# Mask and row maximum of the diagonal score blocks as one VectorE instruction in a fused attention and FP4 feed-forward block

## The chip, the cores and the metric

The kernel runs on one core of a Trainium2 chip. The metric is device time in microseconds (us), median of three runs. A core has TensorE (PE in the profile; PEld is its weight load), VectorE (DVE), ScalarE (ACT), GpSimd (POOL) and SyncE (SP), which here issues the DMAs. SBUF is the working memory; PSUM has the banks into which TensorE writes.

## The reference

A transformer block with both branches on one normalised input; x is 8 x 1024 x 512, with 16 heads of 32 columns.

```python
xn = layernorm(x)
# causal attention
q, k, v = split(xn @ W_attn + b_attn)
att = (q @ k.T) * 32 ** -0.5
att = where(tril, att, -inf)
y   = softmax(att) @ v
a   = y @ W_proj + b_proj
# feed-forward: inputs and weights of each product rounded to blockwise FP4 (16 values a scale)
f   = fp4_linear(silu(fp4_linear(xn, w_gate)) * fp4_linear(xn, w_up), w_down)
out = x + a + f
```

## The kernel before

Tokens are taken in 64 tiles of 128 rows (8 batches of 8 tiles). Attention works in 64 units; a unit is two heads of one batch. Each unit takes two passes. `maxima` computes the scores with queries on the partitions and keeps each row's negated maximum (`neg`) and its sum of exponentials (`row_sums`). `weigh` computes the scores again, transposed (L710 adds the shift from the first pass, L713 the product), exponentiates them (L721), zeroes the masked half of diagonal blocks on POOL (L727) and multiplies by v (L692). Besides, `project` makes q, k and v (L464, L509), `network` is the feed-forward part (L817 products with gate and up, L795 product with down, L834 gating on DVE), `Quantised` rounds to FP4 in steps on DVE (L318 to L342), `transposed` turns the result on TensorE (L349) and copies it out on ACT (L350), and `finish` is the output projection (L922, L927). `weights_quantised` rounds the weights in the first part of the run.

In `maxima` a block is 128 query rows (tile t of the batch; t = 4 Q + i) against up to 512 keys (half h). Where h < Q the block is full, 512 columns, and there is no mask. Where h = Q it is diagonal and has n = (i + 1) x 128 columns, of which only the last 128 need the mask. Diagonal blocks of 128 and 256 columns hold both heads in one bank (`count` 2); those of 384 and 512 columns hold one head. Per unit that makes 8 full blocks and 12 diagonal ones, of 16 heads in all. `kind` says which of three statistics a block belongs to: 0 for Q = h = 0, 1 for the full blocks, 2 for Q = h = 1.

A block goes this way: matmul into a bank (L594); for a diagonal block the addition of the mask to the last 128 columns of each head, in place (L606); maximum over the columns, negated, into `neg` (L608); then `summed` exponentiates the bank in place on ACT with `neg` as bias, and the accumulator gives the row sum (L566). After that the bank is free. Six banks are shared by all parts of the kernel; two more hold the accumulators `y` and `acc`.

The order of all engines' instructions is fixed when the program is built. Each part is a generator; `merge` steps them by a planned clock. `dve`, `act` and `pool` add a planned cost to the time at which that engine is planned to be free. `Banks.take` gives the bank that is planned to be free first, and `expect` and `back` set that time. `Later` puts off an instruction to a due time. Of `maxima` these costs matter: 0.16 + 0.135 per head for the mask addition, 0.16 + 0.00103 per column for the reduce, and `LATE` = 0.6 from there to the exponentials; `yield cost, free["dve"] - QUEUE, 1` holds the next block back while DVE is planned to be more than `QUEUE` = 2 us behind. On the chip the engines run in these orders and wait for each other through semaphores. The planner's own costs are in microseconds, but no time of this document is taken from them.

At the end of a unit the statistics are put together (`least`, `gap`, `stat`), transposed (L641), copied to `statT` (L643) and stored to DRAM by two DMAs (L649, L652).

Of the kernel before, what the change touches and what calls it, by code (L numbers as in the profile page):

```python
# [9 lines left out]
F32 = mybir.dt.float32  # L10
# [4 lines left out]
ALU = mybir.AluOpType  # L15
AX = mybir.AxisListType
# [3 lines left out]
P = 128  # L20
# [3 lines left out]
MASKED = -1e30  # L24
# [3 lines left out]
def kernel(  # L28
# [31 lines left out]
    nc = tc.nc  # L60
# [14 lines left out]
    W = QG * P  # L75
# [17 lines left out]
    const = ctx.enter_context(tc.tile_pool(name="const", bufs=1))  # L93
    p1 = ctx.enter_context(tc.tile_pool(name="p1", bufs=1))
    p2 = ctx.enter_context(tc.tile_pool(name="p2", bufs=2))
# [9 lines left out]

    ident = const.tile([P, P], F32, name="ident")
    make_identity(nc, ident)
    mask = const.tile([P, P], F32, name="mask")
    make_causal_mask(nc, mask, mask_val=MASKED)
    power = const.tile([P, 1], F32, name="power")  # L110
    nc.gpsimd.memset(power, -0.5)

# [30 lines left out]
    def on(engine, us, after=0.0):  # L143

        free[engine] = max(free[engine], clock[0], after + HOP) + us
        return free[engine]

    def act(columns, after=0.0, function="other"):
        if function == "other":
            function = table[0]  # L150
        switch = TABLE if function != table[0] else 0.0
        table[0] = function
        return on("act", 0.17 + 0.00083 * columns + switch, after)

    def dve(us, after=0.0):
        return on("dve", us, after)
# [275 lines left out]
    def settle(entries):  # L432
        while entries:
            entries.pop(0).now()
# [120 lines left out]
    def maxima(un):  # L555

        NK = QG * HU

        neg = p2.tile([P, 3, NK], F32, name="neg")
        sums = p2.tile([P, 3, NK], F32, name="row_sums")  # L560
        older = []

        def summed(bank, sc, n, kind, k, count):
            for j in range(count):
                part = sc[:, j * n : (j + 1) * n]
                nc.scalar.activation(  # L566
                    part,
                    part,
                    AF.Exp,
                    bias=neg[:, kind, k + j : k + j + 1],  # L570
                    accum_out=sums[:, kind, k + j : k + j + 1],
                )
                end = act(n, 0.0, "exp") + 0.27
                free["act"] = end
            banks.back(bank, end)


        blocks = []
        for t in range(NT):
            for h in range(t // QG):  # L580
                blocks += [(t, h, (r,)) for r in range(HU)]
            if t % QG < 2:
                blocks.append((t, t // QG, range(HU)))
            else:
                blocks += [(t, t // QG, (r,)) for r in range(HU)]
        for t, h, heads in blocks:
            Q, i = t // QG, t % QG
            while len(un.qs) <= Q:
                yield 0.0, clock[0] + 0.5, 0
            n = W if h < Q else (i + 1) * P  # L590
            kind, k, count = Q + h, i * HU + heads[0], len(heads)
            bank, sc = banks.take()
            for j, r in enumerate(heads):
                nc.tensor.matmul(  # L594
                    sc[:, j * n : (j + 1) * n],
                    lhsT=un.qs[Q][:, r, i * P : (i + 1) * P],
                    rhs=un.ks[h][:, r, :n],
                    start=True,
                    stop=True,
                )  # L600
            cost = count * max(0.11, n * 0.000444)
            end = clock[0] + cost
            each = sc[:, : count * n].rearrange("p (r c) -> p r c", r=count)
            if h == Q:
                corner = each[:, :, n - P : n]
                nc.vector.tensor_tensor(corner, corner, mask.unsqueeze(1).broadcast_to([P, count, P]), ALU.add)  # L606
                end = dve(0.16 + 0.135 * count, end)
            nc.vector.tensor_reduce(neg[:, kind, k : k + count], each, AX.X, ALU.max, negate=True)  # L608
            end = dve(0.16 + 0.00103 * n * count, end)
            block = (bank, sc, n, kind, k, count)  # L610
            older.append(Later(end - clock[0] + LATE, lambda block=block: summed(*block)))
            banks.expect(bank, end + LATE + 0.6 + 0.4 * count)
            while len(older) > 3:
                older.pop(0).now()
            yield cost, free["dve"] - QUEUE, 1
        yield 0.0, end + LATE + 1.0, 0
        settle(older)

        least = p2.tile([P, NK], F32, name="least")
        nc.vector.tensor_tensor(least, neg[:, 1, :], neg[:, 2, :], ALU.min)  # L620
        gap = p2.tile([P, 2, NK], F32, name="gap")
        for part in range(2):
            nc.vector.tensor_tensor(gap[:, part, :], least, neg[:, 1 + part, :], ALU.subtract)
        yield 0.0, dve(0.6), 0
        nc.scalar.activation(gap, gap, AF.Exp)
        yield 0.0, act(2 * NK, 0.0, "exp"), 0
        nc.vector.tensor_tensor(sums[:, 1:, :], sums[:, 1:, :], gap, ALU.mult)
        nc.vector.tensor_tensor(sums[:, 1, :], sums[:, 1, :], sums[:, 2, :], ALU.add)

        high = p2.tile([P, 2, NK], F32R, name="neg_high")  # L630
        stat = p2.tile([P, 3, 2, HU, QG], F32, name="stat")
        by_head = lambda a: a.rearrange("p (i r) -> p r i", r=HU)
        for q, source in enumerate((neg[:, 0, :], least)):
            nc.vector.tensor_copy(high[:, q, :], source)
            nc.vector.tensor_copy(stat[:, 0, q], by_head(high.bitcast(F32)[:, q, :]))
            nc.vector.tensor_tensor(stat[:, 1, q], by_head(source), stat[:, 0, q], ALU.subtract)
            nc.vector.reciprocal(stat[:, 2, q], by_head(sums[:, q, :]))
        rows = 3 * 2 * NK
        yield 0.0, dve(2.0), 1
        bank, pt = banks.take()  # L640
        nc.tensor.transpose(pt[:rows, :P], stat.rearrange("p e q r i -> p (e q r i)"), ident)  # L641
        statT = p2.tile([rows, P], F32, name="statT")
        nc.scalar.copy(statT, pt[:rows, :P])  # L643
        end = act(P, clock[0] + 0.15)
        banks.back(bank, end)

        def store():
            un.shift = dram.tile([2, 2, HU, W], F32, name="shift_kept")
            nc.sync.dma_start(  # L649
                out=un.shift.rearrange("e q r (i p) -> (e q r i) p", p=P), in_=statT[: 2 * 2 * NK, :]  # L650
            )
            nc.sync.dma_start(  # L652
                out=un.batch.inverses[un.u].rearrange("q r (i p) -> (q r i) p", p=P), in_=statT[2 * 2 * NK :, :]
            )
            Later(3.0, load)

        def load():
            un.shT = shifts[un.n % 2]
            for q in range(2):
                for r in range(HU):  # L660
                    row = (q * HU + r) * HD
                    nc.sync.dma_start(out=un.shT.bitcast(F32)[row : row + 2, :], in_=un.shift[:, q, r, :])
            un.ready = clock[0] + 4.0

        Later(end - clock[0] + 0.5, store)
        yield 0.15, 0.0, 0
# [377 lines left out]
    with tc.manual_schedule(  # L1044
# [25 lines left out]
        part, late = EARLY * 0.25, [0.0]  # L1070
# [18 lines left out]
        def first_maxima():  # L1089
            yield 0.0, clock[0] + 6.0, 1  # L1090
            yield from maxima(units[0])
# [24 lines left out]
        def preparations():  # L1116
            for n in range(AHEAD, N, QT):
# [4 lines left out]
            [  # L1122
                Stream((weigh(un), 17.5, un.n, 1.0) for un in units),
                Stream((maxima(un), 6.0, un.n - 1 - SOONER, 1.0) for un in units[1:]),
                Stream(networks()),
                Stream((quantised(tl), 0.45, tl.n + LAG - 1, 0.5) for tl in tiles),
# [42 lines left out]
```

## Time and profile before

| | |
|---|---|
| median of 3 runs | 4298.45 us (4293.16 to 4298.53) |
| profiled execution | 4298.47 us |
| its span, first to last instruction | 4296.8 us |
| mean granted TensorE clock | 0.990 |
| instructions | 58518 |

A profile page gives the busy time of each engine, and groups of instructions: line, engine, operation, output<-input by the program's names, shapes and count; then, behind the first bar, the busy time and the mean duration in ns of one; behind the second bar the idle time of the engine just ahead of them, and what ended it. A list of waits gives for each pair (who waits <- for whom) the total us, how many times and the longest. Matmuls are pipelined and recorded longer than they occupy the array, so that the rows of PE add up to more than its busy time. Some records are missing: of 768 wide reduces 518.1 / 0.687 = 754 are seen.

### The profile page before, as it was taken

How to read it: one execution, taken by the hardware profiler on the slowest of the kernel's cores; microseconds unless marked ns; L12 is line 12 of the kernel's file. 1: busy time of each engine (PE TensorE's matmuls, PEld its weight loads, DVE VectorE, ACT ScalarE, POOL GpSimd, SP SyncE). 2: the span in 40 equal slices, each digit the busy share in tenths (PEclk: the TensorE clock that was granted, in tenths of full speed). 3: DMA queues.
4: the chain of work that ended last, by engine and by line, in shares of the span. 5: the costliest groups of instructions: out<-in, count | busy, mean ns of one | idle time of the engine just before them, and what ended most of it. 6: DMA issues, size and time to landing. Idle time of an engine off the chain costs nothing.

```text
span 4296.8 us, 58518 instructions
## 1 busy us (share of the span) xinstructions
PE 4145.0 (96%) x17684; PEld 2617.7 (61%) x17684; DVE 2942.0 (68%) x6811; ACT 2331.5 (54%) x5918; POOL 543.8 (13%) x1295
## 2 busy tenths in 40 slices
PE   7779999999999999999999999999999999999998
PEld 6665566666666666666666666666666555555555
DVE  6787766667676667676667676667676777767755
ACT  2246656565555555555555555555555566666640
POOL 0001111111111111111111111111111111111110
PEclk9889999999999999999999999999999999999999
DMA  5654434455454555454455454555454433333314
GB/s 182 173 170 129 123 102 119 118 154 162 130 157 139 141 165 163 126 162 133 140 165 163 127 161 133 143 160 163 128 151 126 114 87 92 92 85 94 94 53 125
DMA packets 564187, 573.85 MB, mean 134 GB/s; under 512 B 114976, under 2 KB 420128, under 8 KB 563872
## 3 DMA queue, kind: packets, MB, share of 16 engines
q1 hardware_dynamic: 563872, 570.10, 47.7%
q8 instruction: 143, 2.34, 0.2%
q14 instruction: 172, 1.41, 0.1%
HBM read 400.56 MB, written 169.35 MB: 133 GB/s over the span
## 4 chain that ended last, share of the span: by engine, by line
PE 80%; DVE 6%; ACT 4%; DMA 3%; issue 2%; SPq 1%; ACTq 0%; POOL 0%; DVEq 0%; POOLq 0%
PE bank L817 25%; PE acc L795 12%; PE bank L464 8%; PE y L692 7%; PE bank L710 6%; PE bank L713 6%; PE bank L922 5%; PE bank L594 4%; PE bank L509 4%; ACT bank L566 3%; PE bank L349 2%; DVE neg L608 2%; DMA inv_y<-inv_kept 1%; DVE scale L333 1%; DMA yT<-y_kept 0%
## 5 line engine op out<-in xcount | busy, mean ns | idle before, releaser
L608 DVE TENSOR_REDUCE neg<-bank 128x1 f32<-128x512 f32 (+3 forms) x1280 | 800.5, 635 | 258.5 <-PE bank L594 232.2
L566 ACT ACTIVATE bank<-bank,neg 128x512 f32<-128x512 f32 (+3 forms) x1536 | 857.9, 559 | 194.3 <-DVE neg L608 154.7
L721 ACT ACTIVATE pr<-bank 128x512 f32<-128x512 f32 (+3 forms) x1536 | 662.1, 495 | 377.0 <-PE bank L713 364.5
L727 POOL TENSOR_SCALAR_AFFINE_SELECT pr<-pr 128x128 f32<-128x128 f32 x1024 | 389.2, 393 | 3109.9 <-ACT pr L721 3103.6
L710 PE MATMUL bank<-shT,pick 128*128 128x512 f32 (+3 forms) x1536 | 678.3, 450 | 14.5 <-DMA shT<-shift_kept 12.3
L817 PE MATMUL bank<-wuT,xqT 128*128 128x512 f32 (+1 forms) x1536 | 672.4, 562 | 10.7 <-ACT bank L566 6.0
L795 PE MATMUL acc<-wdT,hqT 128*128 128x512 f32 x1408 | 665.2, 598 | 1.3 <-ACT hqT L350 1.3
L817 PE MATMUL bank<-wgT,xqT 128*128 128x512 f32 (+1 forms) x1536 | 666.1, 561 | 0.2 <-ACT bank L566 0.2
L594 PE MATMUL bank<-ks,qs 128*128 128x512 f32 (+3 forms) x1536 | 614.3, 467 | 32.6 <-ACT bank L566 29.9
L713 PE MATMUL bank<-qs,ks 128*128 128x512 f32 (+3 forms) x1536 | 516.9, 346 | 0.0
L606 DVE TENSOR_TENSOR bank<-bank,mask 128x128 f32<-128x128 f32 (+1 forms) x768 | 259.1, 337 | 350.2 <-PE bank L594 350.1
L594 PEld LDWEIGHTS bank<-ks,qs 128*128 128x128 f32 x1536 | 274.5, 190 | 243.9 <-issue 104.1
L817 PEld LDWEIGHTS bank<-wuT,xqT 128*128 128x128 f32 x1536 | 275.7, 190 | 211.8 <-issue 138.1
L817 PEld LDWEIGHTS bank<-wgT,xqT 128*128 128x128 f32 x1536 | 281.0, 190 | 195.9 <-issue 138.9
L710 PEld LDWEIGHTS bank<-shT,pick 128*128 128x128 f32 x1536 | 290.0, 189 | 173.9 <-issue 90.1
L476 ACT ACTIVATE full<-bank,bqk 128x256 f32<-128x256 f32 x256 | 107.3, 470 | 516.2 <-PE bank L464 367.5
L795 PEld LDWEIGHTS acc<-wdT,hqT 128*128 128x128 f32 x1408 | 257.5, 191 | 207.0 <-issue 196.6
L713 PEld LDWEIGHTS bank<-qs,ks 128*128 128x128 f32 x1536 | 290.3, 189 | 103.9 <-issue 70.6
L464 PE MATMUL bank<-xnT,wa 128*128 128x256 f32 x1536 | 347.5, 379 | 1.0 <-ACT xnT L350 0.5
L464 PEld LDWEIGHTS bank<-xnT,wa 128*128 128x128 f32 x1536 | 291.2, 190 | 75.7 <-issue 33.2
L692 PE MATMUL y<-pr,vs 128*32 128x512 f32 (+3 forms) x3072 | 315.8, 501 | 2.2 <-POOL pr L727 2.1
L566 ACT ACTIVATION_READ_ACCUMULATOR bank<-bank,neg 128x1 f32 x1536 | 313.3, 204 | 0.0
(97 smaller groups left out, 4539.7 us busy)
## 6 DMA issues: line engine op xcount, KB each, us to landing
wa<-in_L_attn_W_attn_dram SPq DMA_DIRECT2D x146, 512.0 KB
qs<-qk_kept SPq DMA_DIRECT2D x512, 128.0 KB
ks<-qk_kept SPq DMA_DIRECT2D x512, 128.0 KB
wp<-in_L_attn_W_proj_dram SPq DMA_DIRECT2D x81, 512.0 KB
qk_kept<-high SPq DMA_DIRECT2D x128, 256.0 KB
qk_kept<-full SPq DMA_DIRECT2D x128, 256.0 KB
y_kept<-yu SPq DMA_DIRECT2D x256, 128.0 KB
yT<-y_kept SPq DMA_DIRECT2D x112, 256.0 KB
```

What stands on the lines that cost most here:

```text
L464: nc.tensor.matmul(pq[:, j, :], lhsT=halves[j][:, c, :], rhs=xnT[:, c, :], start=(c == 0), stop=(c == NC - 1),)
L566: nc.scalar.activation(part, part, AF.Exp, bias=neg[:, kind, k + j : k + j + 1], accum_out=sums[:, kind, k + j : k + j + 1],)
L594: nc.tensor.matmul(sc[:, j * n : (j + 1) * n], lhsT=un.qs[Q][:, r, i * P : (i + 1) * P], rhs=un.ks[h][:, r, :n], start=True, stop=True,)
L606: nc.vector.tensor_tensor(corner, corner, mask.unsqueeze(1).broadcast_to([P, count, P]), ALU.add)
L608: nc.vector.tensor_reduce(neg[:, kind, k : k + count], each, AX.X, ALU.max, negate=True)
L692: nc.tensor.matmul(y[row : row + HD, q0:], lhsT=un.vs[h][:, jj, r * HD : (r + 1) * HD], rhs=pr[:, q0:], start=(j < 2), stop=(j >= last - 1 ...
L710: nc.tensor.matmul(w[:, q0:], lhsT=pick[:, Q * HU + r, :], rhs=un.shT[:, q0:], start=True, stop=False)
L713: nc.tensor.matmul(w[:, q0:], lhsT=un.ks[h][:, r, jj * P : (jj + 1) * P], rhs=un.qs[Q][:, r, q0:], start=False, stop=True,)
L721: nc.scalar.activation(pr[:, q0:], w[:, q0:], AF.Exp)
L727: nc.gpsimd.affine_select(out=pr[:, q0 : q0 + P], in_=pr[:, q0 : q0 + P], compare_op=ALU.is_ge, fill=0.0, base=0, pattern=[[1, P]], channe ...
L795: nc.tensor.matmul(tl.acc, lhsT=job.hqT[:, j, :], rhs=wdT[:, i, :], start=(i == 0), stop=(i == NI - 1))
L817: nc.tensor.matmul(job.g, lhsT=job.tl.xqT[:, c, :], rhs=wT[:, c, job.i0 : job.i0 + job.w], start=(c == 0), stop=(c == NC - 1),)
```

## The change

The mask becomes 512 columns wide: 384 columns of zeros and then the causal mask of 128. A diagonal block's head then takes one `tensor_tensor_reduce`: it adds the last n columns of the wide mask to the n columns of scores, multiplies by -1, writes this back to the bank, and takes the minimum of it into `neg`, which is the negated row maximum as before. Since the bank now holds negated scores in the diagonal blocks (`kind` 0 and 2), the exponential there takes `scale=-1.0`. Full blocks keep their reduce. The planned cost of a diagonal head is 0.16 + 0.00105 per column. `statT` moves from a pool with two buffers to one with one.

```diff
-    mask = const.tile([P, P], F32, name="mask")
-    make_causal_mask(nc, mask, mask_val=MASKED)
+    mask = const.tile([P, W], F32, name="mask")
+    nc.gpsimd.memset(mask[:, : W - P], 0.0)
+    make_causal_mask(nc, mask[:, W - P :], mask_val=MASKED)
...
                     bias=neg[:, kind, k + j : k + j + 1],
+                    scale=1.0 if kind == 1 else -1.0,
                     accum_out=sums[:, kind, k + j : k + j + 1],
...
-            each = sc[:, : count * n].rearrange("p (r c) -> p r c", r=count)
             if h == Q:
-                corner = each[:, :, n - P : n]
-                nc.vector.tensor_tensor(corner, corner, mask.unsqueeze(1).broadcast_to([P, count, P]), ALU.add)
-                end = dve(0.16 + 0.135 * count, end)
-            nc.vector.tensor_reduce(neg[:, kind, k : k + count], each, AX.X, ALU.max, negate=True)
-            end = dve(0.16 + 0.00103 * n * count, end)
+                for j in range(count):
+                    part = sc[:, j * n : (j + 1) * n]
+                    nc.vector.tensor_tensor_reduce(
+                        part,
+                        part,
+                        mask[:, W - n :],
+                        scale=-1.0,
+                        scalar=3e38,
+                        op0=ALU.add,
+                        op1=ALU.min,
+                        accum_out=neg[:, kind, k + j : k + j + 1],
+                    )
+                    end = dve(0.16 + 0.00105 * n, end)
+            else:
+                nc.vector.tensor_reduce(neg[:, kind, k : k + 1], sc[:, :n], AX.X, ALU.max, negate=True)
+                end = dve(0.16 + 0.00103 * n, end)
...
-        statT = p2.tile([rows, P], F32, name="statT")
+        statT = p1.tile([rows, P], F32, name="statT")
```

## The prediction

> **What bounds the kernel now.** I read the busy shares first, then the chain of work that ended last.
>
> ```profile
> span 4296.8 us, 58518 instructions
> ...
> PE 4145.0 (96%) x17684; PEld 2617.7 (61%) x17684; DVE 2942.0 (68%) x6811; ACT 2331.5 (54%) x5918; POOL 543.8 (13%) x1295
> ...
> PE 80%; DVE 6%; ACT 4%; DMA 3%; issue 2%; SPq 1%; ACTq 0%; POOL 0%; DVEq 0%; POOLq 0%
> ```
>
> TensorE (PE) is busy 4145 of 4297 us and carries 80% of the chain. VectorE (DVE), which the change works on, is busy 68%. So DVE time saved is worth nothing by itself; it is worth what PE stops waiting. The table of busy time by stage tells where PE waits:
>
> ```profile
> 0.00:107.00 107.00, 84.89 (x391) 73.04 (x392) 72.37 (x165) 24.63 (x51) 8.64 (x23) 0.97 0.58 182
> 107.00:215.00 108.00, 79.51 (x368) 69.17 (x367) 79.50 (x178) 24.77 (x58) 3.56 (x6) 0.84 0.61 174
> 215.00:322.00 107.00, 83.43 (x375) 64.82 (x377) 91.90 (x213) 48.69 (x138) 6.49 (x16) 0.89 0.57 170
> ...
> 1000.00:2000.00 1000.00, 989.68 (x4272) 628.32 (x4271) 679.37 (x1583) 565.15 (x1433) 133.07 (x309) 1.00 0.53 149
> 2000.00:3000.00 1000.00, 990.92 (x4261) 630.07 (x4260) 677.99 (x1573) 562.65 (x1429) 137.14 (x320) 1.00 0.54 150
> ```
>
> After start and length the columns are PE, weight loads, DVE, ACT (ScalarE), POOL. In the steady part PE idles about 10 us per 1000. All PE idle time in the span is 4296.8 - 4145.0 = 152 us, 74 of it in the first 322 us. No saving can go much above that. What PE waits for, from the list of waits:
>
> ```profile
> ACT bank L566 <- DVE neg L608: 154.7, 161, 3.0
> ...
> PEld bank L594 <- ACT bank L566: 89.9, 208, 3.3
> ...
> PE bank L594 <- ACT bank L566: 29.9, 93, 2.9
> ```
>
> This is the changed path: a score block is written to a PSUM bank (L594), masked (L606) and reduced (L608) on DVE, exponentiated in place on ACT (L566), and only then may PE write that bank again. PE's matmuls idle 29.9 us for it at L594 and, in smaller rows, 6.1 at L817 and about 2 elsewhere: 38 us. Its weight loads wait some 150 us on the same release (89.9 at L594, 29.7, 13.8, 11.1 and 8.6 elsewhere), most of it while an earlier matmul still streams.
>
> **The change part by part.** The DVE rows it touches, by shape:
>
> ```profile
> L608 DVE TENSOR_REDUCE neg<-bank 128x1 f32<-128x512 f32 x768 | 518.1, 687 | 240.9 <-PE bank L594 232.2
> ...
> L606 DVE TENSOR_TENSOR bank<-bank,mask 128x128 f32<-128x128 f32 x512 | 150.1, 293 | 197.2 <-PE bank L594 197.2
> ...
> L608 DVE TENSOR_REDUCE neg<-bank 128x1 f32<-128x384 f32 x256 | 142.7, 558 | 8.7
> ...
> L606 DVE TENSOR_TENSOR bank<-bank,mask 128x256 f32<-128x256 f32 x256 | 109.0, 426 | 153.0 <-PE bank L594 153.0
> ...
> L608 DVE TENSOR_REDUCE neg<-bank 128x2 f32<-128x512 f32 x128 | 88.5, 692 | 4.4
> ...
> L608 DVE TENSOR_REDUCE neg<-bank 128x2 f32<-128x256 f32 x128 | 54.3, 424 | 4.4
> ```
>
> *Removed.* All 768 mask additions, 259.1 us. The reduces of diagonal blocks: 142.7 + 88.5 + 54.3, and of the 768 wide reduces the 256 on diagonal blocks, 256 x 0.687 = 175.9. Together 720.5 us. The other 512 wide reduces stay.
>
> *Added.* One fused instruction per head and diagonal block: 16 for each of the 64 units (two heads of one batch), 256 each of 128, 256, 384 and 512 columns. The built program shows each as two DVE instructions, the streaming one and a one-column write of the accumulator into `neg`; so DVE gets 2048 + 512 instead of 768 + 1280 of these, 512 more. Neither is in the trace. For the streaming one the nearest rows also take one PSUM and one SBUF input: L606 at 128 columns 0.293, L927 at 256 0.416, L834 at 384 and 512 0.550 and 0.682, in sum 1.941, times 256 = 496.9 us. For the accumulator write the nearest is the one-column L398, 0.154: 1024 x 0.154 = 157.7. Sum 654.6 us, **66 us of DVE less** (2942 to about 2876). Bounds: a write that hides behind its stream costs 0, making 224 less. ACT's own accumulator read (204 ns at L566), with the 65 ns by which the accumulating 512-column L566 exceeds the plain L721 (666 against 601), gives 0.269 x 1024 = 275 and DVE 52 us more. If the fused form streamed at half rate, 256 x 1280 columns more at about 1.04 ns (L834, 132 ns for 128 columns) add 341: 275 us more. I take 0.154: same engine, one column, while L566's is another engine's.
>
> [...]
>
> *Path of one diagonal block.* Before: addition, a gap of 0.04 in the timeline, reduce: 0.29 + 0.04 + 0.69 = 1.02 us at 512 columns, 0.89 at 384, 1.16 and 0.89 for pairs of 256 and 128. After: 0.84, 0.70, 1.14, 0.89. Only the single-head blocks get shorter, by 0.18, and ACT and the bank follow. In each pair the second fused instruction waits for the first's accumulator write (a semaphore in the built program); behind it in DVE's queue stand the quantiser's steps, delayed by no more than the 0.04 that the removed wait cost.
>
> *The order.* The planner priced the old diagonal path at 0.98 for a 512 block (measured 1.02) and prices the new one at 0.16 + 0.00105 n, 0.70. So all queues come out in another order. In the built programs PE has the same matmuls, with 5829 instead of 5738 changes from line to line; weighting each kind of change by its mean delay in this trace gives 459 us instead of 465, so -6. Pricing PE's work between a score block's matmul and the next write to its bank by the trace's back-to-back matmuls (0.43 us for 512 fp32 columns, 0.23 for 512 fp32r), 100 of 1280 blocks get their bank rewritten within 2.5 us before, 35 after. The bank path needs about 2 us (1.02, then 0.67 + 0.20 on ACT, and hops), so these are the reuses on which PE waits. Fewer by 65 in 100: of the 38 us 25 go; were the weight loads' 150 us all exposed, 122 would. I take 25, near the lower end, as loads overlap matmuls.
>
> *Given back.* The plan is too early by what it does not price: 0.84 - 0.70 = 0.14 us for each of 1024 fused pairs, 143 us of lateness, against 0.04 x 768 = 31 before. Lateness reaches PE where the bank is wanted soon: 101 of 1280 reuses lie within 3.5 us, 8%, so 0.08 x 112 = 9 us; as ACT's queue is in order and the releases of other banks stand behind a late exponential, I add as much as half again, 4. Together 0.12 x 112 = 13. Ends: 0, and 112 x 0.25 = 28, where 0.25 is PE's 38 us over ACT's 154.7 us of waiting for L608.
>
> *At nothing.* POOL's additional fill of 384 columns at the start is about 0.4 us (L115's 512 take 0.52) and is covered by DVE's first wait for `xt`, 14.3 us; without it, 0.4. `scale` -1 on L566 is an immediate in the same instruction. `statT` with one buffer instead of two makes L643 wait for the previous unit's two stores, one unit (about 64 us) earlier; both lie 5 us behind L643 in the trace, and if uncovered would cost those 5 us per unit. Table loads stay 187.
>
> **Sum.** On the profiled 4298.47 us (span 4296.8 and 1.67 around it; the median is 4298.45, so no correction): -25 - 6 + 13 = -18. **4280 us**.
>
> **Rivals.** *The wait moves.* PE's floor is its own work; a removed wait is found again at another line in front of a PE at 99%. For it speaks the steady part's 10 us per 1000, against it the fewer tight reuses. Without the 25, -6 and +13 are left; at an unpriced few us either way I call it 0: 4298. *DVE saves nothing, the order still helps.* With 0.269 per accumulator write the lateness is 0.255 a block, 261 us, 230 over before: -31 + 0.12 x 230 = -3, or with the 8% alone -13; 4290. For it speaks ACT's row, against it that ACT is another engine. *Slower: the fused instruction streams at half rate* and DVE becomes late. Lateness is then 0.14 + 0.33 on average, 481 us, 450 over before; with the 0.25 share +113, with 12% +54, less 31: +23 to +82, likeliest +50, 4348 us. DVE would stand at 75%. It turns the sign where lateness times share passes 31 us: at the 12% share from (31 / 0.12 + 31) / 1024 = 0.28 us per block, twice my estimate. For it speaks that no row shows such an instruction; against it that L606 and L834 already stream two inputs at full rate.
> [...]
> *Also slower*: the new order itself puts a wait elsewhere (a quantiser step late on DVE, so its transposes L349 late on PE: 30.8 us in 6 waits before, almost all in the first stage); twice those waits give +30 - 18 = +12, 4310.
>
> **How the numbers follow.** Forecast 0.45, wait moved 0.17, DVE saves nothing 0.10, half rate 0.12, order worse 0.16. A measurement of this kernel can tell about 0.2%, 8.6 us, from no change. Faster: 0.45 and half of the 0.10, 0.50. Same: the 0.17 and the other 0.05, 0.22. Slower: 0.28. The low end: all 38 us of bank waits gone, the 6, nothing given back, and 12 of the loads' 150 us: -56, 4242. The high end takes in the order rival and the lower part of the half-rate one: 4335. The forecast's own range is 4242 to 4289.
>
> **What would show it.** Right: DVE near 2876 us, PE's idle behind L566 near 15 instead of 38, PE busy unchanged within 15. The streaming instruction at 512 columns near 0.68 and its accumulator write near 0.15 decide the price. Wrong: a 512-column stream over 1 us, or unchanged ACT bank waits, or more PE idle in front of L349 or L692.

## The result, and the profile after

| | before | changed |
|---|---|---|
| median, same chip | 4297.34 us (4293.16 to 4298.53) | 4256.54 us (4251.42 to 4260.17) |
| profiled execution, span | 4298.47, 4296.8 us | 4251.42, 4249.7 us |

The ratio is 0.9906, 95% interval 0.9893 to 0.9919: 41 us faster where 18 were forecast. Direction and range held; the size did not. The comparisons further down were made on other chips, whose medians for the kernel before lie between 4293.7 and 4301.0, so they are given as ratios; 0.001 is 4.3 us.

The profile page of the changed kernel, busy times and chain (its lines are shifted: L568 is the old L566, L597 the old L594, L724 the old L710):

```profile
span 4249.7 us, 58555 instructions
...
PE 4131.2 (97%) x17684; PEld 2619.1 (62%) x17684; DVE 2763.2 (65%) x7323; ACT 2321.8 (55%) x5918; POOL 546.5 (13%) x1296
...
PE 82%; ACT 7%; DVE 4%; DMA 1%; issue 1%; SPq 0%; ACTq 0%; POOL 0%; DVEq 0%
```

DVE has 512 instructions more and is busy 179 us less. PE is busy 13.8 us less with the same matmuls (the mean granted clock, 0.991 instead of 0.990, accounts for an estimated 0.001 x 4250 = 4 of that), and idle 4249.7 - 4131.2 = 118.5 us instead of 151.8. The table of busy time by stage, same columns as before:

```profile
0.00:107.00 107.00, 84.22 (x394) 72.98 (x395) 73.31 (x168) 24.79 (x52) 8.64 (x24) 0.97 0.59 184
107.00:215.00 108.00, 78.32 (x373) 68.33 (x372) 80.00 (x185) 25.28 (x59) 4.68 (x8) 0.87 0.62 175
215.00:322.00 107.00, 86.71 (x390) 65.93 (x389) 90.53 (x239) 52.23 (x147) 6.49 (x17) 0.87 0.56 171
...
1000.00:2000.00 1000.00, 996.24 (x4310) 632.77 (x4309) 635.00 (x1710) 560.36 (x1432) 135.28 (x314) 1.00 0.53 149
2000.00:3000.00 1000.00, 996.10 (x4277) 631.92 (x4276) 635.90 (x1703) 569.05 (x1452) 133.31 (x311) 1.00 0.54 151
```

PE now idles 4 us per 1000 in the steady part instead of 10. By the copies of `y` (two a unit on ACT, in the traces' order of time, units counted from 0), unit 8 begins to be copied out 10 us sooner (761 against 771), unit 48 26 us sooner (3304 against 3330), the last unit 57 us sooner (4098.5 against 4155.5). The very last copy comes 45 us sooner (4127 against 4172), and what follows it, feed-forward products and output projections, takes 122 us instead of 125. So the gain is spread over the run, and thickest in the last 15 units, where a unit takes about 53 us instead of 54 to 55.

The groups of the fused instruction, busy and mean as before:

```profile
L610 DVE CUSTOM_DVE_ANT_0 bank<-bank,mask 128x512 f32<-128x512 f32 x256 | 175.4, 701 | 99.7 <-PE bank L597 98.6
L610 DVE DVE_READ_ACCUMULATOR2_ANT neg<- 128x1 f32 x1024 | 144.6, 141 | 0.1
L610 DVE CUSTOM_DVE_ANT_0 bank<-bank,mask 128x384 f32<-128x384 f32 x256 | 142.9, 570 | 110.8 <-PE bank L597 110.3
L610 DVE CUSTOM_DVE_ANT_0 bank<-bank,mask 128x256 f32<-128x256 f32 x256 | 110.9, 433 | 37.6 <-PE bank L597 33.1
...
L610 DVE CUSTOM_DVE_ANT_0 bank<-bank,mask 128x128 f32<-128x128 f32 x256 | 76.1, 297 | 221.5 <-PE bank L597 213.6 <-ACT pr L735 3.6
```

The streams took 0.701, 0.570, 0.433 and 0.297 us; the forecast had 0.682, 0.550, 0.416 and 0.293. There is no half rate. The accumulator write is recorded at 0.141, near the 0.154 taken, yet it costs almost nothing, as the timeline of DVE shows (start, duration):

```profile
1511.64 0.56 DVE L610 CUSTOM_DVE_ANT_0 bank<-bank,mask 128x384 f32<-128x384 f32 x1
1512.11 0.14 DVE L610 DVE_READ_ACCUMULATOR2_ANT neg<- 128x1 f32 x1
1512.11 0.68 DVE L335 TENSOR_REDUCE scale<-hid 128x32 f32<-128x512 f32 x1
...
1503.12 0.14 DVE L610 DVE_READ_ACCUMULATOR2_ANT neg<- 128x1 f32 x1
1503.30 0.43 DVE L610 CUSTOM_DVE_ANT_0 bank<-bank,mask 128x256 f32<-128x256 f32 x1
```

The write starts before its stream's record ends (1511.64 + 0.56 = 1512.20), and the next instruction starts with it. It shows where the next one waits for it, above all at the second of a pair: 0.18 from its start to the next start. With the old cost of 720.5, a fall of 178.8 leaves 541.7 for the diagonal blocks; the streams, 256 x 2.001 = 512, leave 29 us, 0.03 per write.

PE's own waits, who waits <- for whom, total us, times, longest:

```profile
PE bank L597 <- ACT bank L568: 21.7, 55, 2.3
...
PE bank L655 <- DVE stat L651: 4.8, 1, 4.8
...
PE bank L724 <- ACT bank L568: 1.1, 2, 0.6
PE bank L831 <- ACT bank L568: 1.0, 4, 0.3
```

Behind the score banks PE idles 24 us instead of 38. Two waits of the end of a unit, which the forecast had not counted, also shrank: for the statistics to 4.8, and for the shift's load into `shT`, which is gone. The kernel before had

```profile
PE bank L641 <- DVE stat L637: 12.6, 9, 5.1
PE bank L710 <- DMA shT<-shift_kept: 12.3, 7, 3.1
```

These three, 14, 8 and 12 us, are about the whole 33 us by which PE idles less; with the 14 us of busy time they make the 47 us between the two spans. ACT's own waits for the maxima, on the other hand, are nearly what they were, 119.8 + 30.6 = 150.4 us instead of 154.7:

```profile
ACT bank L568 <- DVE neg L610: 119.8, 90, 2.8
...
ACT bank L568 <- DVE neg L622: 30.6, 34, 2.4
```

### The profile page after: what moved, and what is told of

It reads as the page before. It is cut to its first block, busy times and chain, and to the rows that moved or that the text cites. A ratio compares the mean times of both kernels' runs of the same rounds, so it can differ in the third digit from the quotient of the medians.

```text
span 4249.7 us, 58555 instructions
## 1 busy us (share of the span) xinstructions
PE 4131.2 (97%) x17684; PEld 2619.1 (62%) x17684; DVE 2763.2 (65%) x7323; ACT 2321.8 (55%) x5918; POOL 546.5 (13%) x1296
## 4 chain that ended last, share of the span: by engine, by line
PE 82%; ACT 7%; DVE 4%; DMA 1%; issue 1%; SPq 0%; ACTq 0%; POOL 0%; DVEq 0%
PE bank L831 26%; PE acc L809 12%; PE bank L466 8%; PE y L706 7%; PE bank L724 6%; PE bank L727 6%; PE bank L597 5%; PE bank L936 5%; PE bank L511 4%; ACT bank L568 3%; PE bank L351 2%; ACT L568 1%; ACT L843 1%; ACT pr L735 1%; DMA ks<-y_kept 1%
## 5 line engine op out<-in xcount | busy, mean ns | idle before, releaser
L568 ACT ACTIVATE bank<-bank,neg 128x512 f32<-128x512 f32 (+3 forms) x1536 | 856.7, 559 | 163.7 <-DVE neg L610 119.8
L610 DVE CUSTOM_DVE_ANT_0 bank<-bank,mask 128x128 f32<-128x128 f32 (+3 forms) x1024 | 501.2, 500 | 469.5 <-PE bank L597 455.7
L724 PE MATMUL bank<-shT,pick 128*128 128x512 f32 (+3 forms) x1536 | 683.8, 453 | 2.7 <-DVE hid L848 1.5
L597 PE MATMUL bank<-ks,qs 128*128 128x512 f32 (+3 forms) x1536 | 636.2, 475 | 24.7 <-ACT bank L568 21.7
L622 DVE TENSOR_REDUCE neg<-bank 128x1 f32<-128x512 f32 x512 | 345.7, 685 | 186.8 <-PE bank L597 185.6
L597 PEld LDWEIGHTS bank<-ks,qs 128*128 128x128 f32 x1536 | 277.5, 191 | 234.1 <-issue 111.3
L724 PEld LDWEIGHTS bank<-shT,pick 128*128 128x128 f32 x1536 | 290.4, 189 | 155.7 <-issue 78.9
L568 ACT ACTIVATION_READ_ACCUMULATOR bank<-bank,neg 128x1 f32 x1536 | 315.4, 205 | 0.0
```

The costliest lines, as they stand in the source:

```text
L568: nc.scalar.activation(part, part, AF.Exp, bias=neg[:, kind, k + j : k + j + 1], scale=1.0 if kind == 1 else -1.0, accum_out=sums[:, kind, ...
L597: nc.tensor.matmul(sc[:, j * n : (j + 1) * n], lhsT=un.qs[Q][:, r, i * P : (i + 1) * P], rhs=un.ks[h][:, r, :n], start=True, stop=True,)
L610: nc.vector.tensor_tensor_reduce(part, part, mask[:, W - n :], scale=-1.0, scalar=3e38, op0=ALU.add, op1=ALU.min, accum_out=neg[:, kind, k ...
L622: nc.vector.tensor_reduce(neg[:, kind, k : k + 1], sc[:, :n], AX.X, ALU.max, negate=True)
L724: nc.tensor.matmul(w[:, q0:], lhsT=pick[:, Q * HU + r, :], rhs=un.shT[:, q0:], start=True, stop=False)
```

## The experiments

The question: where do the other 23 us come from? **Theory A**: from the order, since a cheaper plan of the diagonal blocks redraws all queues. **Theory B**: from the shorter path of a block on the chip, at 512 columns about 0.75 instead of 1.02 us (stream and the end of its accumulator write). Two kernels take one each. They have, on PE, ACT and SP, exactly the order of the one kernel and the instructions of the other.

**The fused instruction in the order of before**

The edit is against the changed kernel; the first new line stands behind the loop over the heads.

```diff
-                    end = dve(0.16 + 0.00105 * n, end)
+                end = dve(0.16 + 0.135 * count, end)
...
-                end = dve(0.16 + 0.00103 * n, end)
+            end = dve(0.16 + 0.00103 * n * count, end)
```

> The fused instruction with the planned costs of the kernel before, so that every queue but VectorE's has the order of the kernel before. Theory A (the gain is the new order): within 10 us of the kernel before, some 4290, with PE still idle some 30 us behind L566 at L594. Theory B (the gain is the shorter path of a block, about 0.74 instead of 1.02 us at 512 columns): most of the 41 us, some 4265, and PE's idle behind the exponential near 20.

Measured 4292.06 us, ratio 0.9994 (0.9985 to 1.0003). DVE was busy 2780.0 us, 162 less than before, and that was worth nothing that can be measured. PE still idled behind the exponentials as before:

```profile
PE bank L597 <- ACT bank L568: 30.1, 93, 3.3
...
PE bank L724 <- DMA shT<-shift_kept: 11.1, 7, 2.4
```

**Mask addition and reduce in the order of the changed kernel**

This edit is against the kernel before.

```diff
-                end = dve(0.16 + 0.135 * count, end)
...
-            end = dve(0.16 + 0.00103 * n * count, end)
+            if h == Q:
+                for j in range(count):
+                    end = dve(0.16 + 0.00105 * n, end)
+            else:
+                end = dve(0.16 + 0.00103 * n, end)
```

> Mask addition and reduce as before, but planned at the fused instruction's cost, so that every queue but VectorE's has the order of the changed kernel. Theory A: 4265 to 4275, most of the gain without the fused instruction. Theory B: 4297 or slower. A third theory, that the two need each other: 4300 to 4320, since each diagonal block is about 0.28 us later than planned, 0.28 x 768 = 215 us of lateness, of which 8 to 12% reach the end.

Measured 4271.11 us, 0.9943 (0.9930 to 0.9957): 24 us of the gain without the fused instruction, against a plan that is wrong for what runs. PE's waits have the look of the changed kernel; none for `shT` is left:

```profile
PE bank L594 <- ACT bank L566: 22.3, 54, 2.7
```

The wait for the statistics is 7.0 us here. So B falls as the main cause and A holds, with this one pair of orders; whether the cheaper plan or chance made the new order better is asked below. But the fused instruction is worth something in an order made for it: 0.9943 to 0.9906 is 16 us, by the two intervals 8 to 24.

**Lateness priced**

```diff
+                    nc.vector.tensor_copy(extra, part[:, 0:1])
                     nc.vector.tensor_tensor_reduce(
```

The changed kernel gets a copy of one column of the block, to a tile of its own, ahead of each fused instruction.

> The changed kernel in its own order, with one more unplanned one-column copy from the block's bank on VectorE ahead of each fused instruction (1024, about 0.12 to 0.15 us each, 120 to 155 us of lateness). It prices lateness: by the 8 to 12% of the prediction 10 to 19 us slower than the changed kernel (4267 to 4275), by the 25% of its upper end 30 to 39 us (4287 to 4295). If lateness is absorbed by idle VectorE time: within 4 us.

Measured 4273.03 us, 0.9951 (0.9938 to 0.9963), 16 to 19 us slower than the changed kernel (medians, ratios). The copies take

```profile
L611 DVE COPY extra<-bank 128x1 f32<-128x1 f32 x1024 | 157.8, 154 | 405.3 <-PE bank L598 395.5
```

so 10 to 12% of unplanned DVE time on this path reaches the end; the intervals of the two ratios leave 7 to 17%. The 16 us above fit the same share: DVE was busy 2927.1 - 2763.2 = 164 us longer in the separate form.

**The storage alone**

```diff
+    wide_mask = const.tile([P, W], F32, name="mask")
+    nc.gpsimd.memset(wide_mask[:, : W - P], 0.0)
+    make_causal_mask(nc, wide_mask[:, W - P :], mask_val=MASKED)
+    mask = wide_mask[:, W - P :]
...
-        statT = p2.tile([rows, P], F32, name="statT")
+        statT = p1.tile([rows, P], F32, name="statT")
```

> The kernel before with the 512-column mask (its last 128 columns are used) and the single-buffered statT. Every theory: within 5 us of the kernel before. If the single buffer or the moved tiles matter, some other time: 5 us per unit would give 4600.

Measured 4294.87 us, 1.0001 (0.9992 to 1.0010). Wide mask and single buffer cost nothing, as forecast.

**What makes an order good?** Three kernels change only the planned cost of the fused instruction, to 0.20, 0.08 and 0.40 in place of 0.16, one the limit at which `maxima` holds its next block back.

```diff
-                    end = dve(0.16 + 0.00105 * n, end)
+                    end = dve(0.20 + 0.00105 * n, end)
```

> The changed kernel with the planned cost of a fused instruction at 0.20 + 0.00105 n, which at 512 columns is the 0.74 us that the trace of the changed kernel shows, instead of 0.16 + 0.00105 n. Theory truth (the order gets better the nearer the plan is to the chip): 4250 to 4256. Theory reuse (the time goes with the number of score banks that PE's order rewrites within 2.5 us of its own work, 100 before and 35 after; the fused instruction in the two orders gives 35.5 us for 65 of them, 0.55 us each): 86 of them here, so 4284. Theory luck: anything between 4250 and 4292.

Measured 4245.07 us, 0.9880 (0.9865 to 0.9895).

> The same with 0.08 + 0.00105 n, below what the chip takes. Truth: slower than the changed kernel by the added lateness, 0.08 x 1024 = 82 us at the 0.105 that the late run showed, 9 us, 4265, or more. Reuse: 57 tight reuses, 12 us more than the changed kernel, 4268. Luck: anything.

Measured 4265.98 us, 0.9931 (0.9918 to 0.9943).

> The same with 0.40 + 0.00105 n, as dear as mask addition and reduce were at 512 columns. Truth: as the fused instruction in the order of before, about 4292. Reuse: 106 tight reuses, 4295. Luck: anything.

Measured 4276.81 us, 0.9956 (0.9943 to 0.9968).

```diff
-    QUEUE = 2.0
+    QUEUE = 1.5
```

> The changed kernel with QUEUE at 1.5 instead of 2.0 us: a unit's next score block is held back when VectorE is planned to be over 1.5 us behind. 44 tight reuses (35 in the changed kernel) and 5796 changes of line on PE (5830). Reuse: 5 us more by the reuses, 5 less by the changes of line: 4256, equal to the changed kernel within 5. Luck: anything.

Measured 4215.94 us, 0.9814 (0.9800 to 0.9827).

The count of tight reuses (counted in the built programs), on which the forecast's 25 us rested, falls as a predictor: with 86 of them `0.20` beats the changed kernel with 35, and with 44 `QUEUE` 1.5 beats it by 40 us. Among the four planned costs the one that is nearest to the chip is the fastest, and the time rises to both sides (0.08: 0.9931, 0.16: 0.9906, 0.20: 0.9880, 0.40: 0.9956), by steps no larger than those of a draw (below), so that this is not shown to be a rule.

**Or the draw?** `HOP`, the planned hand-over from one engine to the next, is changed in both kernels by an amount that means nothing: from 0.20 to 0.21, then to 0.19 and 0.22. Every instruction stays; all orders are drawn anew.

```diff
-    HOP = 0.2
+    HOP = 0.21
```

> The kernel before with the planner's HOP (the planned hand-over from one engine to the next) at 0.21 instead of 0.20 us: every instruction the same, all orders redrawn by a change that means nothing. Theory price (the order improved because the plan of the diagonal blocks got cheaper): within 8 us of the kernel before. Theory lottery (any change of a planned number redraws the order, and the time moves by some 20 us either way): 4270 to 4320.

> The changed kernel with HOP at 0.21. Price: within 8 us of the changed kernel's 4256. Lottery: 4235 to 4280.

> The kernel before with HOP 0.19. Lottery: anywhere in 4260 to 4330. Price: 4290 to 4305.

> The changed kernel with HOP 0.19. If the cheaper plan and the fused instruction are worth some 30 us on the mean of the draws: 4240 to 4270. If the 41 us were the draw: up to 4290.

> The kernel before with HOP 0.22. Lottery: anywhere in 4260 to 4330. Price: 4290 to 4305.

> The changed kernel with HOP 0.22. If the cheaper plan and the fused instruction are worth some 30 us on the mean of the draws: 4240 to 4270. If the 41 us were the draw: up to 4290.

| HOP | kernel before | changed kernel |
|---|---|---|
| 0.19 | 4307.61 us, 1.0026 (1.0016 to 1.0035) | 4235.70 us, 0.9859 (0.9845 to 0.9872) |
| 0.20 | 1 | 0.9906 (0.9893 to 0.9919) |
| 0.21 | 4272.86 us, 0.9946 (0.9933 to 0.9958) | 4249.38 us, 0.9886 (0.9871 to 0.9901) |
| 0.22 | 4284.58 us, 0.9962 (0.9949 to 0.9974) | 4249.25 us, 0.9876 (0.9861 to 0.9891) |
| mean | 0.9984 | 0.9882 |

Price and lottery, the two theories of these runs, both had a part. Redrawing the order of the kernel before moves it by up to 23 us down and 11 up, as much as the whole forecast. Yet in all four pairs the changed kernel is ahead, by 26 to 72 us, on the mean by 0.0102 or 44 us. The 41 us are near this mean and no lucky draw. From the spread of four pairs the mean is known only to some 30 us either way.

**The fused instruction in two more fixed orders**, that of the kernel before with `HOP` 0.21 and that of the changed kernel with `QUEUE` 1.5; edits as in the first two experiments, with that number.

> The fused instruction in the order of the kernel before with HOP 0.21 (4273). If a plan that is too dear for the fused instruction hides its gain, as in the order of before: 4270 to 4273. If it is worth the 0.105 that the late run showed for each us of VectorE lateness, with 0.28 us over 768 blocks, 215 us: 4250.

Measured 4278.18 us, 0.9953 (0.9940 to 0.9967), against 0.9946 with the separate form: no gain.

> Mask addition and reduce in the order of the changed kernel with QUEUE 1.5 (4216 with the fused instruction). If the fused instruction is worth what it was in the changed kernel's order, 15 us: 4231. If a tighter order needs it more: 4240 to 4270.

Measured 4235.04 us, 0.9859 (0.9845 to 0.9872), against 0.9814: the fused instruction is worth 19 us there. So in two orders planned for the slow form it is worth nothing, in two planned for the fast form 16 and 19 us:

| order of | mask addition and reduce | fused instruction |
|---|---|---|
| kernel before | 1 | 0.9994 |
| kernel before, `HOP` 0.21 | 0.9946 | 0.9953 |
| changed kernel | 0.9943 | 0.9906 |
| changed kernel, `QUEUE` 1.5 | 0.9859 | 0.9814 |

**QUEUE with the other plans**

> The kernel before with QUEUE at 1.5 instead of 2.0. If the shorter queue is good by itself, as with the changed kernel (4216 against 4256, 40 us): 4257. If it is good only with the fused instruction or by the draw: 4285 to 4310.

Measured 4354.10 us, 1.0134 (1.0120 to 1.0147): the same edit that gives the changed kernel 40 us costs the kernel before 58. It also gives a second price of the plan alone: with `QUEUE` 1.5 the separate form takes 1.0134 in the order of before and 0.9859 in that of the changed kernel, 119 us (an estimated 40 of it in the granted clock, see below).

> The changed kernel with QUEUE at 1.5 and the measured path, 0.20 + 0.00105 n. If the two gains (40 and 11 us) add: 4205. If each is a draw of the order: 4225 to 4260.

Measured 4232.04 us, 0.9847 (0.9834 to 0.9861): the two gains do not add. `QUEUE` 1.5 with the change as it is, 4215.94 us, is the fastest kernel of the study, 1.9% under the kernel before; whether 1.5 is a better limit or a good draw these runs do not settle. Its PE idles 1 us per 1000 in the steady part:

```profile
1000.00:2000.00 1000.00, 999.12 (x4343) 638.02 (x4342) 643.57 (x1722) 568.87 (x1459) 130.38 (x315) 1.00 0.55 152
```

Across several kernels one line goes with the time, PE's idle ahead of the score matmuls behind the exponentials: 41.9 us at 1.0026 (`HOP` 0.19 before), 29.9 at 1, 22.3 at 0.9943, 21.7 at 0.9906, 13.0 at 0.9859 and 7.1 at 0.9814. From the first to the last of these 34.8 us of idle go with 0.0212, 91 us, of time, 2.6 to one. It is a tendency, with exceptions (28.9 us at 0.9946, `HOP` 0.21 before; 11.7 at 0.9880, `0.20`; 30.4 at 0.9956, `0.40`).

Part of the time beyond the idle us is in the granted clock. On the mean of its executions it lies between 0.988 and 0.991 for all kernels but three: 0.986 with `HOP` 0.19 before and with `0.40`, 0.980 with `QUEUE` 1.5 before. The last one's trace shows where the clock falls, in stretches of 3.4 us (the shortest whole stretches at half clock in the traces of the kernel before and of the changed kernel last 3.41 us):

```profile
1744.10:1747.50 3.40, 3.40 (x15) 1.93 (x13) 1.00 (x2) 3.36 (x9) 0.00 (x0) 1.00 0.00 0
1747.50:1750.90 3.40, 1.97 (x7) 0.82 (x5) 3.33 (x8) 3.22 (x11) 0.00 (x0) 0.99 0.20 77
1750.90:1754.30 3.40, 3.40 (x7) 2.35 (x8) 3.30 (x8) 3.00 (x10) 0.00 (x0) 0.50 0.00 0
1754.30:1757.70 3.40, 3.40 (x17) 2.92 (x16) 0.81 (x4) 0.77 (x2) 0.00 (x0) 1.00 0.00 0
```

PE idles 1.4 of the 3.4 us behind the exponentials, and the next 3.4 us run at half clock (0.50, the third number from the right). In this trace all 23 stretches at half clock between 400 and 4100 us follow 3.4 us in which PE idled 0.9 us or more. In the traces of the kernel before and of the changed kernel there are 5 and 1 between these times, behind 0.96 us of idle or more. Not every such idle is followed by one (cut at the same step, 15 and 7 stretches of 3.41 us idle 0.9 us or more there), and what decides it is open. As an estimate, if PE's work sets the time throughout, the clock missing against 0.990 is worth 0.010 x 4354 = 44 of the 58 us that `QUEUE` 1.5 costs the kernel before, 17 of the 20 us by which `0.40` is behind `0.16`, and more than the 11 us of `HOP` 0.19. The changed kernel has the 0.990 of the kernel before on the mean, so its 41 us aren't from there. What PE's busy time holds besides, up to some 40 us between these kernels, was not separated.

## Why the prediction was right or wrong

- **PE bounds, DVE time is worth only what PE stops waiting**: right, and more strictly than put: 162 us of DVE saved in the old order gave 2 us, within the noise.
- **Streams at full rate, mask and `statT` at nothing, `scale` free**: right. L568's mean is 559 ns as before. The half-rate rival is dead for one PSUM and one SBUF source: the stream took 0.701 us at 512 columns, where the sign of it was over 1 us.
- **Accumulator write, 1024 x 0.154 = 158**: wrong size, about 29. DVE fell by 179, toward the low bound of 224, not by 66. The price was the duration of a one-column record; this write's record lies almost wholly within those of its stream and of the next instruction (in the timeline above it runs from 1512.11 to 1512.25, the stream to 1512.20, the next from 1512.11). The fused form has 512 DVE instructions more, accumulator writes included, and DVE is busy 179 us less. Without the writes it has 512 fewer.
- **Given back, +13**, the first step that failed: the share was right within the noise (12%, measured 10 to 12), the lateness was not. With 0.03 for the write the fused instruction holds DVE for 0.73 us at 512 columns, and ACT may start after about 0.75, against a plan of 0.70: 30 to 50 us in all, against 31 before, at 12% at most +2. Without this error the sum is -31 + 2 = -29, 4269 us. This is about half of the miss.
- **-25 for fewer tight reuses**, the second step that failed: the place was in part right, the way to size it was not. PE's own idle there fell by 14 us, not 23, while 12 and 8 us vanished at `shT` and the statistics, waits that the sum left at nothing without a reason. Both belong to the order: in the old one with the fused instruction they stay (11.1 and 11.7 us), in the new one with the separate form they are gone and 7.0. PE's busy time fell by 14 more, an estimated 4 of it by the clock; the rest stays open. The count itself does not rank orders. The separate form in the new order, with all its lateness, gave 24 us.
- **-6 for PE's changes from line to line**: no run shows this term by itself. PE's busy time, which fell by 14, is within the 15 that the forecast allowed.
- **The signs**: DVE near 2876 us (2763 measured) and PE's idle behind L566 near 15 (24) did not come; the write's 0.15 came as a record (0.141), but its cost is 0.03 and it did not decide the price. ACT's waits for the maxima, 150 us instead of 155, come near one sign of being wrong, and this fits: the shorter path of a block was not the main gain.
- **The range**, 4242 to 4335, held the time although the draw of an order alone turned out to be worth some 20 us to either side, so this holding is partly luck. The order rival was right that a new order can be slower (`QUEUE` 1.5 with the old plan, 58 us), but there the wait grew at the score banks (43.0 us instead of 29.9) and not at the quantiser's transposes (31.3 instead of 30.8), and it was wrong for this order (32.6).

## What to carry to other kernels

Where a planner fixes the queues when the program is built, an instruction is worth little until the plan knows its cost: here 0 us in two orders made for the slow form, 16 and 19 in two made for the fast one. The price in the plan alone was worth 24 us in one pair of orders and 119 in another, so its size differs widely from order to order. Before a change of some 20 us in such a kernel is believed or refused, redraw the order by a planned number that means nothing, in both kernels, and compare the draws. And price a new instruction's tail by what its neighbours can hide, not by the duration of the nearest row (here about 0.03 us, against 0.154).

## What the runs showed of the hardware that was not expected

The fused add-and-minimum with accumulator takes 0.297, 0.433, 0.570 and 0.701 us for 128 to 512 fp32 columns, in place in PSUM with the mask in SBUF: 4 to 20 ns more than plain two-input instructions of the kernel before (0.293, 0.416, 0.550 and 0.682). Its accumulator write is recorded at 141 ns, but the next VectorE instruction starts with it unless it waits for it, so that it costs about 0.03 us.

Half clock came behind PE's own waits: with `QUEUE` 1.5 before, each of the 23 stretches at half the granted clock between 400 and 4100 us follows 3.4 us in which PE idled 0.9 us or more, and the mean clock is 0.980 instead of 0.990. In the stretch shown, 1.4 us of idle stand ahead of 3.4 us at 0.50, which is an estimated 1.7 us of clock missing. By that, such a wait can cost more than its own time.
